# Three of the eight weight sums of a product by thirds move from VectorE to GpSimd

## The chip, the core and the metric

The kernel runs on one core of a Trainium2 chip. Its engines are TensorE (PE in the profile; PEld are its weight loads), VectorE (DVE), ScalarE (ACT), GpSimd (POOL) and SyncE (SP), each with a queue of its own that it works through in order, and 16 DMA engines that all queues share. [...] The metric is the device time of one execution in microseconds (us), the median of several runs.

## What is computed

A graph network of two attention layers over 512 nodes with 768 features and 16,896 edges (8,192 drawn edges, the same turned round, and 512 loops), then a residual and a normalisation:

```python
def gat_layer(x, W, a_s, a_d, b, edge_index, concat):
    n = x.shape[0]
    H, C = a_s.shape
    h = (x @ W).reshape(n, H, C)
    src, dst = (edge_index[0], edge_index[1])
    alpha_s = jnp.einsum('nhc,hc->nh', h, a_s)
    alpha_d = jnp.einsum('nhc,hc->nh', h, a_d)
    e = jax.nn.leaky_relu(alpha_s[src] + alpha_d[dst], NEG_SLOPE)
    m = jax.ops.segment_max(e, dst, num_segments=n)
    e = jnp.exp(e - m[dst])
    denom = jax.ops.segment_sum(e, dst, num_segments=n)
    alpha = e / (denom[dst] + EPS)
    msg = h[src] * alpha[:, :, None]
    out = jax.ops.segment_sum(msg, dst, num_segments=n)
    out = out.reshape(n, H * C) if concat else out.mean(axis=1)
    return out + b
...
h = gat_layer(x, W1, a_src1, a_dst1, b1, edge_list, concat=True)   # 8 heads of 768
h = jax.nn.elu(h)
out = gat_layer(h, W2, a_src2, a_dst2, b2, edge_list, concat=True) # 1 head
...
x = _layernorm(x + out, axis=-1)
```

All data is float32.

## The kernel before

The edges become a dense 512 x 512 matrix of counts, so that attention is a masked softmax over a full matrix and the sum over edges a matrix product. Heads of layer 1 are numbered 0 to 7. For each head the kernel multiplies x by that head's 768 columns of W1 (tiles `hs`), forms the attention matrix (tiles `q`, then `PT`), multiplies it with `hs` (the aggregation), applies ELU (tile `gT`) and multiplies the result by that head's 768 rows of W2, which adds into `h2`. The heads overlap: while head h is aggregated and multiplied by its part of W2, head h+2 is multiplied by its part of W1.

Three schemes with fewer multiplications are used. The aggregation of heads 1 to 5 splits each float32 number into a high and a low part: ScalarE makes the high part (`aH`, L996), VectorE the low part (`aL`, L1000) and their difference (`aD`, L1004), all in tiles named `room`, and TensorE multiplies them (L1044, L1052). Other products are done by quarters. The products with W1 for heads 2 to 7 and with W2 for heads 1 to 7 are done *by thirds*: the 768 x 768 weight is cut in nine blocks of 256 x 256, and fifteen sums and differences of blocks, named P0 to P14, are each multiplied once (W1 products: operations `M.P0` to `M.P14`, L473, emptied into `hs` at L481; W2 products: `m.P0` to `m.P14`, L553, emptied into `h2` at L561).

Of the fifteen weight operands some are raw blocks, some are made by a load on SyncE's queue (L190 for rows, L184 for a block) and an adding DMA on GpSimd's queue (L187: `P1`, `P14`, `P13`, `P12`, `P11`), and eight are made by arithmetic, at L200 in the function `load_thirds`. W1 uses the tiles `w2r` and `w2t`, W2 the tiles `w1r` and `w1t` (swapped for the last head). Each of the eight works on two blocks of 128 x 512 numbers, float32, in SBUF:

- P6 = P14 - P4, then P4 = P13 + P4, P2 = P12 - P13, P10 = P5 + P1, P0 = P12 + P0,
- P1 = P6 + P1, P3 = P10 - P3 and P7 = P6 + P7. P1 overwrites an operand of P10, so it also comes after P10.

There are twelve full sets of eight (six for W1, in the scripts `T.P6` and so on, and six for W2, `w.P6` and so on), and four more in the last head, where the other four sums are made by adding DMAs from SBUF to SBUF (L203).

The order of everything is written by hand. `HEAD`, `REST` and `END` are strings of names, one string for each head, and `run` calls the functions of that name one after the other; each engine's queue then holds its share in that order. Nothing is reordered afterwards. `SPLIT_HEAD` serves heads 1 to 4. Where it makes the sums for W2, it reads:

```python
        dst0 w.P10 A4 D1 aD4 k4 G0 aH2 D4 aH5 w.P6 aL2 aD2 w.P0 d.p12 A2 aL5 v3 v1 G3 aD5 w.P4 k2 v4 w.P1 A5 rooms
        w.P3 G1 G4 m.P2 w.P7 g.P12 k5 D2 D5 v2 dst1 v5 g.P9 swap e.P2 buffers g.P7 d.r3 d.P12 lift2 lift0 next lift1
```

Here `A2` and `A5` are matmuls (L1044) that read what `aH` and `aL` of the same number made, `D` the matmuls (L1052) that read `aD`, `G` writes `gT` (L1061), and `d.P12` is an adding DMA of GpSimd.

Of the kernel before, what the change touches and what calls it, by code (L numbers as in the profile page):

```python
# [37 lines left out]
def gat_pass(  # L38
# [16 lines left out]
    nc = tc.nc  # L55
# [74 lines left out]
    def weight_tile(name, shape):  # L130
        if name not in kept_tiles:
            kept_tiles[name] = wpool.tile([P, *shape], F32, name=name)
        return kept_tiles[name]
# [21 lines left out]
    def square(t_, j):  # L155
        return t_[:, j * 2 * TH:(j + 1) * 2 * TH].rearrange("p (k n) -> p k n", k=2)

    def load_thirds(slot, m, apart):

        def of(rows, k):  # L160
            return rows[k:k + HK + 1:HK] if apart else rows[2 * k:2 * k + 2]

        chunks = list(range(DC))

        def third(k, n):
            ks = of(chunks, k)
            return rows_[:, ks[0]:ks[1] + 1:ks[1] - ks[0], n * TH:(n + 1) * TH]

        def part(k, n):
            cols = slice(n * TH, (n + 1) * TH)  # L170
            if apart:
                return m[:, cols].rearrange("(j k p) d -> k p j d", j=2, p=P)[k]
            return m[k * TH:(k + 1) * TH, cols].rearrange("(k p) d -> p k d", p=P)

        def flat(j):
            return weight_tile(shape=(HK, HALF), name=f"{slot}t{j}").rearrange("p k n -> p (k n)")

        rows_, pair_ = weight_tile(shape=(DC, D), name=f"{slot}r"), flat(1)
        two, four = flat(2), flat(4)
        P13, P12, P11 = square(pair_, 0), square(pair_, 1), square(four, 0)  # L180
        add = ALU.add

        def load(o, k, n):
            return lambda: nc.sync.dma_start(o, part(k, n))  # L184

        def join(o, k, n):
            return lambda: nc.gpsimd.dma_start(o, part(k, n), accum_op=add)  # L187

        def row(k):
            return lambda: nc.sync.dma_start(rows_[:, k, :], m[k * P:(k + 1) * P, :])  # L190

        loads = {f"r{k}": row(k) for k in range(DC)}
        loads.update(P1=join(third(1, 1), 1, 2), P14=join(third(2, 1), 0, 1), p13=load(P13, 0, 2), P13=join(P13, 2, 2),
                     p12=load(P12, 0, 0), P12=join(P12, 1, 0), p11=load(P11, 0, 1), P11=join(P11, 1, 1))
        raw = {(k, n): third(k, n) for k in range(3) for n in range(3)}
        B_ = dict(P8=raw[0, 2], P9=raw[0, 0], P5=raw[0, 1], P13=P13, P12=P12, P14=raw[2, 1], P4=raw[2, 0], P0=raw[1, 2],
                  P3=raw[2, 2], P7=raw[1, 0], P1=raw[1, 1], P6=square(two, 0), P2=square(two, 1), P11=P11, P10=square(four, 1))

        def op(o, a, b, how):
            return lambda: nc.vector.tensor_tensor(B_[o], B_[a], B_[b], op=how)  # L200

        def onto(o, a):
            return lambda: nc.gpsimd.dma_start(B_[o], B_[a], accum_op=add)  # L203
        return B_, loads, dict(
            P6=op("P6", "P14", "P4", ALU.subtract), P4=op("P4", "P13", "P4", add), P2=op("P2", "P12", "P13", ALU.subtract),
            P10=op("P10", "P5", "P1", add), P0=op("P0", "P12", "P0", add), P1=op("P1", "P6", "P1", add),
            P3=op("P3", "P10", "P3", ALU.subtract), P7=op("P7", "P6", "P7", add),
            **{f"q{o}": onto(o, a) for o, a in (("P0", "P12"), ("P4", "P13"), ("P1", "P6"), ("P7", "P6"))})

# [73 lines left out]
    for j in range(2):  # L283
        nc.vector.tensor_reduce(picks[:, j:j + 1], ident.rearrange("p (j k) -> p k j", k=32)[:, j, :], axis=AX.X,
                                op=ALU.add)
# [30 lines left out]
    else:  # L316
# [5 lines left out]
        for c in range(EC):  # L322
            m = (c + 0.5) * P * N / E
            b = int(m // B)
# [1335 lines left out]
```

## Time and profile before

| | before |
|---|---|
| median of 3 runs | 603.82 us (602.72 to 603.88) |
| profiled execution | 604.01 us, span 602.2 us |
| granted TensorE clock, mean | 0.996 |
| TensorE busy | 594.0 us |
| VectorE busy | 534.3 us |
| ScalarE busy | 323.6 us |
| GpSimd busy | 99.0 us, 139 instructions |

The span runs from the first instruction of the program to the last; the time of the execution holds 1.8 us more. "Busy" is the time in which an engine had an instruction; in a row of the timeline stand the start in us from the span's start, the duration, the engine, the line of the kernel, the operation, the tiles written and read, and how many are merged in that row; brackets name the idle time in front of it and what ended it. In rows of groups stand the busy time, the mean of one and the idle time in front.

### The profile page before, as it was taken

To read this page: it belongs to the slowest core of one execution; us is meant where nothing else is said; L and a number is where in the kernel's file an instruction comes from. 1 tells how busy PE (TensorE), PEld (TensorE's weight loads), DVE (VectorE), ACT (ScalarE), POOL (GpSimd) and SP (SyncE) were. 2 spreads that over 40 slices of the span, in tenths; PEclk is the share of its full clock that TensorE was granted. 3 is DMA by queue.
4 is the path that set the end of the run, shared out by engine and by line. 5 is a ranking of instruction groups with operands and counts; after the bars stand their busy time and mean duration, and the time that the engine had idled before them with its cause. 6 is when DMAs were issued, how large, how long until landed. Compare 5 with 4: busy or idle time off the path is not lost.

```text
span 602.2 us, 8248 instructions
## 1 busy us (share of the span) xinstructions
PE 594.0 (99%) x2752; PEld 480.5 (80%) x2752; DVE 534.3 (89%) x1043; ACT 323.6 (54%) x555; POOL 99.0 (16%) x139
## 2 busy tenths in 40 slices
PE   9999999999999999999999999999999999999995
PEld 5666685688888878888888878888888888887863
DVE  7979979768999899988999899989998899899985
ACT  3118774743748164842748255752826347744743
POOL 2210103022012210123011220122021204022000
PEclk9999999999999999999999999999999999999998
DMA  8982899699478977699569987599576959495202
GB/s 296 319 182 71 236 224 278 170 324 223 110 178 191 266 183 208 109 289 213 143 172 179 290 179 214 98 279 233 184 192 166 249 99 257 71 235 98 52 19 107
DMA packets 97341, 114.21 MB, mean 190 GB/s; under 512 B 42966, under 2 KB 78222, under 8 KB 96398
## 3 DMA queue, kind: packets, MB, share of 16 engines
q1 hardware_dynamic: 75230, 89.26, 48.3%
q0 software_dynamic: 21632, 23.79, 25.4%
q10 hardware_dynamic: 432, 0.59, 0.3%
q8 instruction: 23, 0.38, 0.2%
q14 instruction: 24, 0.20, 0.1%
HBM read 99.05 MB, written 2.90 MB: 169 GB/s over the span
## 4 chain that ended last, share of the span: by engine, by line
PE 99%; DVE 0%; ACT 0%; issue 0%; DVEq 0%; ACTq 0%
PE mm L553 23%; PE mm L473 18%; PE mm L414 11%; PE mm L1044 7%; PE mm L1080 5%; PE tr L473 5%; PE bc L553 5%; PE mm L1052 4%; PE tr L553 3%; PE bc L473 3%; PE mm L1475 2%; PE bc L1080 2%; PE tr L1080 2%; PE mm L663 1%; PE bc L1044 1%; PE tr L1044 1%
## 5 line engine op out<-in xcount | busy, mean ns | idle before, releaser
L187 POOL DMA_DIRECT2D w2t<-in_L_gnn_W_dram x21 | 28.4, 1451 | 170.6 <-DMA w2t<-in_L_gnn_W_dram 82.1
L561 DVE TENSOR_TENSOR h<-h,mm 128x512 f32<-128x512 f32 x72 | 49.0, 681 | 8.1 <-PE mm L553 8.0
L703 ACT ACTIVATE q<-q,nmax 128x512 f32<-128x512 f32 x36 | 25.9, 721 | 52.0 <-DVE nmax L700 52.0
L479 ACT ACTIVATE hs<-mm 128x512 f32<-128x512 f32 x23 | 13.6, 593 | 58.5 <-PE mm L473 58.3
L553 PE MATMUL mm<-w1r,gT 128*128 128x256 f32 x176 | 40.4, 379 | 0.0
L928 ACT COPY pS<-q 128x1024 uint16<-128x1024 uint16 x36 | 37.5, 1045 | 0.9
L481 DVE TENSOR_TENSOR hs<-hs,mm 128x512 f32<-128x512 f32 x39 | 26.5, 684 | 12.3 <-PE mm L473 12.1
L553 PE MATMUL mm<-w1r,room 128*128 128x256 f32 x160 | 37.5, 379 | 0.0
L553 PEld LDWEIGHTS mm<-w1r,gT 128*128 128x128 f32 x176 | 33.4, 190 | 4.6
L553 PEld LDWEIGHTS mm<-w1r,room 128*128 128x128 f32 x160 | 30.4, 190 | 4.1
L187 POOL DMA_DIRECT2D w2r<-in_L_gnn_W_dram x14 | 18.6, 1532 | 85.4 <-DVE rden L910 44.0
L187 POOL DMA_DIRECT2D w1t<-in_L_gnn_W_dram x18 | 23.9, 1479 | 45.9 <-DMA w1t<-in_L_gnn_W_dram 39.4
L473 PE MATMUL mm<-w2r,gT 128*128 128x256 f32 x136 | 31.3, 379 | 0.0
L423 DVE SCALAR_TENSOR_TENSOR scr<-hs,a_s 128x768 bf16<-128x768 f32 x32 | 30.5, 953 | 0.4
L423 DVE SCALAR_TENSOR_TENSOR scr<-hs,a_d 128x768 bf16<-128x768 f32 x32 | 30.4, 951 | 0.3
L473 PE MATMUL mm<-w2r,xT 128*128 128x256 f32 x128 | 30.2, 379 | 0.0
L473 PEld LDWEIGHTS mm<-w2r,gT 128*128 128x128 f32 x136 | 25.8, 190 | 3.5
L934 ACT COPY uw<-zr 128x1024 uint16<-128x1024 uint16 x20 | 22.5, 1156 | 9.8 <-DMA zr<-pS 9.8
L473 PEld LDWEIGHTS mm<-w2r,xT 128*128 128x128 f32 x128 | 24.3, 190 | 4.0
L1000 DVE SCALAR_TENSOR_TENSOR room<-room,hs 128x512 fp32r<-128x512 f32 x30 | 20.7, 691 | 7.0 <-ACT room L996 6.8
L695 DVE SCALAR_TENSOR_TENSOR q<-q 128x512 f32<-128x512 f32 x36 | 24.2, 685 | 0.9 <-ACT q L691 0.8
L700 DVE CUSTOM_DVE_ANT_0 q<-q,cnt 128x512 f32<-128x512 f32 x36 | 24.7, 685 | 0.3
(415 smaller groups left out, 1554.7 us busy)
## 6 DMA issues: line engine op xcount, KB each, us to landing
w2r<-in_L_gnn_W_dram SPq DMA_DIRECT2D x48, 384.0 KB
w1r<-in_L_gnn_W_dram SPq DMA_DIRECT2D x43, 384.0 KB
gT<-xd SPq DMA_DIRECT2D x6, 1280.0 KB
w2t<-in_L_gnn_W_dram SPq DMA_DIRECT2D x21, 256.0 KB
w2t<-in_L_gnn_W_dram POOLq DMA_DIRECT2D x21, 256.0 KB, 5.5
w1t<-in_L_gnn_W_dram SPq DMA_DIRECT2D x18, 256.0 KB
w1t<-in_L_gnn_W_dram POOLq DMA_DIRECT2D x18, 256.0 KB, 8.5
w2r<-in_L_gnn_W_dram POOLq DMA_DIRECT2D x14, 256.0 KB, 5.8
```

Of the source, the lines that this page charges most:

```text
L187: return lambda: nc.gpsimd.dma_start(o, part(k, n), accum_op=add)
L414: nc.tensor.matmul(ps[:, :HALF], A_[p][:, k, i * P:(i + 1) * P], B_[p][:, k, :], start=start and k == 0, stop=k == HK - 1, skip_group_chec ...
L423: return [lambda al=al, a=a, sign=sign: nc.vector.scalar_tensor_tensor(scr, HS[h][:, t, :], sign, a, op0=ALU.mult, op1=ALU.mult, accum_out ...
L473: nc.tensor.matmul(bank[chain][:, i * TH:(i + 1) * TH], A_[p][:, k, i * P:(i + 1) * P], B_[p][:, k, :], start=first and i == k == 0, stop= ...
L481: nc.vector.tensor_tensor(out(o), out(o), ps, op=how)
L553: nc.tensor.matmul(bank[chain][:, i * TH:(i + 1) * TH], A_[p][:, k, i * P:(i + 1) * P], B_[p][:, k, :], start=first and i == k == 0, stop= ...
L561: nc.vector.tensor_tensor(out(o), out(o), ps, op=how)
L700: nc.vector.tensor_tensor_reduce(out=q, in0=q, in1=cnt[:, t, :], scale=1.0, scalar=-NO_EDGE / 2, op0=ALU.add, op1=ALU.min, accum_out=nmax)
L703: nc.scalar.activation(q, q, AF.Exp, bias=nmax, scale=-1.0, accum_out=dens[t])
L928: nc.scalar.copy(apart.rearrange("p (h n) -> p h n", h=2), q.bitcast(U16).rearrange("p (n h) -> p h n", h=2))
L1044: nc.tensor.matmul(st["z"][:, :N], A_[c][:, a, s], B_[b][:, s], start=n == s == 0, stop=n == 1 and s == NT - 1, skip_group_check=True)
L1080: nc.tensor.matmul(st[bank][:, :HN], A_[p][:, k, c * P:(c + 1) * P], B_[p][:, k, :], start=start and k == 0, stop=k == 1, skip_group_check ...
```

## The change

Within `load_thirds`, the sums for P1, P3 and P7 are given to GpSimd's queue, at the same places of the hand-written order. The other five stay with VectorE.

```diff
         def op(o, a, b, how):
-            return lambda: nc.vector.tensor_tensor(B_[o], B_[a], B_[b], op=how)
+            engine = nc.gpsimd if o in by_gpsimd else nc.vector
+            return lambda: engine.tensor_tensor(B_[o], B_[a], B_[b], op=how)
+
+        by_gpsimd = ("P1", "P3", "P7")
```

The change adds three lines, so what was L200 is L201, L1000 is L1003, and so on. Two places show what it does to the queues. First GpSimd's queue around the sums for W2 and for W1 of head 1. The tiles `w1t_248` and `w2t_317` hold P6 and P2, `w1t_249` and `w2t_318` hold P11 and P10. Before:

```order
L187 DMA w1r<-in_L_gnn_W_dram 128x2x256 x2
L187 DMA w2t_306<-in_L_gnn_W_dram 128x2x256 x2
L187 DMA w2r<-in_L_gnn_W_dram 128x2x256 x2
L187 DMA w2t_318<-in_L_gnn_W_dram 128x2x256
L187 DMA w1t_118<-in_L_gnn_W_dram 128x2x256 x2
```

and now:

```order
L187 DMA w1r<-in_L_gnn_W_dram 128x2x256 x2
L187 DMA w2t_306<-in_L_gnn_W_dram 128x2x256
L201 TENSOR_TENSOR w1r<-w1t_248,w1r 128x2x256
L201 TENSOR_TENSOR w1r<-w1t_249,w1r 128x2x256
L201 TENSOR_TENSOR w1r<-w1t_248,w1r 128x2x256
L187 DMA w2t_306<-in_L_gnn_W_dram 128x2x256
L187 DMA w2r<-in_L_gnn_W_dram 128x2x256 x2
L201 TENSOR_TENSOR w2r<-w2t_317,w2r 128x2x256
L201 TENSOR_TENSOR w2r<-w2t_318,w2r 128x2x256
L201 TENSOR_TENSOR w2r<-w2t_317,w2r 128x2x256
L187 DMA w2t_318<-in_L_gnn_W_dram 128x2x256
L187 DMA w1t_118<-in_L_gnn_W_dram 128x2x256 x2
```

P1, P3 and P7 of W2 stand between the two adding DMAs into `w2t_306` (P13 and P12 of W1), and P7, P3 and P1 of W1 in front of the adding DMA into `w2t_318` (P11 of W1). Second, VectorE's queue at the first of these places, from P6 on. Before:

```order
L200 TENSOR_TENSOR w1t_248<-w1r 128x512
L1000 SCALAR_TENSOR_TENSOR room<-room,hs 128x512
L1004 TENSOR_TENSOR room<-room 128x512
L200 TENSOR_TENSOR w1r<-w1t_118,w1r 128x2x256
L1000 SCALAR_TENSOR_TENSOR room<-room,hs 128x512
L1061 SCALAR_TENSOR_TENSOR gT<-nr,bc 128x512
L1004 TENSOR_TENSOR room<-room 128x512
L200 TENSOR_TENSOR w1r<-w1t_118,w1r 128x2x256
L200 TENSOR_TENSOR w1r<-w1t_248,w1r 128x2x256
L200 TENSOR_TENSOR w1r<-w1t_249,w1r 128x2x256
L1061 SCALAR_TENSOR_TENSOR gT<-nr,mm_96 128x512
```

and now:

```order
L201 TENSOR_TENSOR w1t_248<-w1r 128x512
L1003 SCALAR_TENSOR_TENSOR room<-room,hs 128x512
L1007 TENSOR_TENSOR room<-room 128x512
L201 TENSOR_TENSOR w1r<-w1t_118,w1r 128x2x256
L1003 SCALAR_TENSOR_TENSOR room<-room,hs 128x512
L1064 SCALAR_TENSOR_TENSOR gT<-nr,bc 128x512
L1007 TENSOR_TENSOR room<-room 128x512
L201 TENSOR_TENSOR w1r<-w1t_118,w1r 128x2x256
L1064 SCALAR_TENSOR_TENSOR gT<-nr,mm_96 128x512
```

From P6 to P4 VectorE's queue is the same; P1 and P3 behind P4 are gone, and P7 a little later.

## The prediction

> **What bounds the kernel now.** I read the page's busy shares first, then the chain that ended last, then busy time by stretches of the span. Two lines of the page:
>
> ```profile
> PE 594.0 (99%) x2752; PEld 480.5 (80%) x2752; DVE 534.3 (89%) x1043; ACT 323.6 (54%) x555; POOL 99.0 (16%) x139
> PE 99%; DVE 0%; ACT 0%; issue 0%; DVEq 0%; ACTq 0%
> ```
>
> The chain is TensorE (PE) from end to end. The stretches say where the missing per cent lies (columns: width, then busy time and count of PE, PEld, DVE, ACT, POOL, granted clock, DMA share, GB/s):
>
> ```profile
> 0.00:10.00 10.00, 8.72 (x32) 5.38 (x33) 7.17 (x17) 2.46 (x4) 3.02 (x57) 1.00 0.79 264
> 140.00:208.00 68.00, 68.00 (x311) 58.38 (x310) 62.72 (x122) 37.54 (x60) 9.38 (x8) 1.00 0.76 196
> 414.00:484.00 70.00, 70.00 (x320) 59.98 (x320) 63.35 (x121) 34.69 (x55) 13.61 (x12) 1.00 0.78 198
> 577.00:602.00 25.00, 18.30 (x60) 10.76 (x59) 18.04 (x43) 9.03 (x20) 0.00 (x0) 0.92 0.17 65
> ```
>
> In the body TensorE is busy all the time at the full clock; its idle time is 1.3 us at the start and 6.7 us in the last 25 us, where no weight sum stands. So nothing taken from VectorE (DVE) can shorten the run by more than crumbs. What can lengthen it is a VectorE result that comes late, and VectorE is 92% busy there (62.72 of 68).
>
> **What the change moves, and its price.** The weight sums as grouped by operation (nanoseconds: minimum, median, maximum):
>
> ```profile
> L200 DVE TENSOR_TENSOR w2r<-w2t,w2r x31: 681/684/693, 115.4 to 554.3; 128x512 f32<-128x512 f32 x31
> L200 DVE TENSOR_TENSOR w1r<-w1t,w1r x30: 650/683/691, 155.0 to 524.9; 128x512 f32<-128x512 f32 x30
> ```
>
> These 61 write into the loaded rows: five sums (P0, P1, P3, P4, P7) in each of twelve sets, and one P3 in the last set. P1, P3 and P7 move: 3 x 12 + 1 = 37. VectorE issues such sums 0.60 us apart (below), so it is relieved of 37 x 0.60 = 22 us; on the path that is worth nothing, since TensorE is what covers it. No DMA is added or removed. The next loads of the rows now also wait for GpSimd's sums, but already waited for the matmuls that read those sums later: nothing.
>
> **GpSimd's price for one sum** is not in the trace: it does no such arithmetic. Nearest rows (GpSimd, by shape; busy us, mean ns, idle before):
>
> ```profile
> L275 POOL IOTA nodes<- 128x512 f16 x1 | 0.6, 553 | 0.4 <-POOLq L1646 0.4
> masks.py:199 POOL TENSOR_SCALAR_AFFINE_SELECT ident<-ident 128x128 f32<-128x128 f32 x1 | 0.3, 294 | 0.1
> L1646 POOL MEMSET const-float32-1.0<- 128x1 f32 x1 | 0.1, 93 | 0.0
> ```
>
> Lower end: VectorE's own 0.68 us. Upper end: the select reads one input, (294 - 93) / 128 = 1.57 ns an element; if each of two inputs cost that, 512 elements take 0.09 + 2 x 0.80 = 1.70 us. I take the middle, 1.2 us. [...]
>
> **Interference between the two engines** is the second unknown, since in the trace GpSimd only fills, generates and issues while VectorE adds. Lower end: VectorE notices nothing. Upper end: a VectorE instruction that comes while a GpSimd sum runs waits for its end. Which one holds decides the sign, because of these rows (VectorE in order of time in head 1, first half; then TensorE):
>
> ```profile
> 153.03 0.68 DVE L200 TENSOR_TENSOR w1t<-w1r 128x512 f32<-128x512 f32 x1
> 153.63 0.69 DVE L1000 SCALAR_TENSOR_TENSOR room<-room,hs 128x512 fp32r<-128x512 f32 x1
> 154.36 0.69 DVE L1004 TENSOR_TENSOR room<-room 128x512 fp32r<-128x512 f32 x1
> 154.97 0.68 DVE L200 TENSOR_TENSOR w1r<-w1t,w1r 128x512 f32<-128x512 f32 x1
> 155.57 0.69 DVE L1000 SCALAR_TENSOR_TENSOR room<-room,hs 128x512 fp32r<-128x512 f32 x1
> 156.17 0.68 DVE L1061 SCALAR_TENSOR_TENSOR gT<-nr,bc 128x512 f32<-128x512 f32 x1
> 156.77 0.69 DVE L1004 TENSOR_TENSOR room<-room 128x512 fp32r<-128x512 f32 x1
> 157.37 1.89 DVE L200 TENSOR_TENSOR w1r<-w1t,w1r 128x512 f32<-128x512 f32 x3
> 160.37 0.68 DVE L200 TENSOR_TENSOR w1r<-w1t,w1r 128x512 f32<-128x512 f32 x1
> ...
> 155.66 1.07 PE L1044 MATMUL tr<-PT,room 128*128 128x512 f32 x4
> 156.57 1.07 PE L1044 MATMUL tr<-pS,room 128*128 128x512 f32 x4
> ```
>
> The first row is P6, the three in one row are P4, P1, P3, the last is P7. P1 and P7 need P6, P3 needs P10, made earlier. VectorE gets to P1, P3 and P7 only at 158 to 161, but GpSimd has nothing else to do and starts P1 as soon as P6 is there, at about 153.7, with P3 and P7 behind it. That is in the middle of the low parts and differences (L1000, L1004), and the L1000 that ends at 155.57 + 0.69 = 156.26 is awaited by the matmul at 156.57: a margin of 0.31 us. With the upper end, P1 starts when the L1000 of 153.63 ends (154.32), ends at 155.52, and the L1004 of 154.36 starts 1.16 us late; nothing has yet been taken from VectorE in front of it. TensorE then stalls 1.16 - 0.31 = 0.85 us, say 0.9. Heads 2 to 4 run the same order; head 4:
>
> ```profile
> 361.13 0.68 DVE L1000 SCALAR_TENSOR_TENSOR room<-room,hs 128x512 fp32r<-128x512 f32 x1
> ...
> 362.10 1.07 PE L1044 MATMUL mm<-pS,room 128*128 128x512 f32 x4
> ```
>
> The margin is again 0.29 us. **Four stalls: 3.6 us.** P3 and P7 collide later, but by then VectorE skips P1, P3, P7 (1.8 us) and catches up.
>
> [...]
>
> Second halves of heads 1 to 4 (the W1 sums): P6 starts at 185.56, and VectorE later idles for TensorE:
>
> ```profile
> 185.56 0.69 DVE L200 TENSOR_TENSOR w2t<-w2r 128x512 f32<-128x512 f32 x1
> 188.70 0.68 DVE L200 TENSOR_TENSOR w2t<-w2r 128x512 f32<-128x512 f32 x1
> 192.32 0.69 DVE L481 TENSOR_TENSOR hs<-hs,mm 128x512 f32<-128x512 f32 x1 [1.04 <-PE mm L473]
> ```
>
> Two collisions cost at most 2.4 us; P7 and P3 leave VectorE (1.2 us) and 1.04 us of idle time follow. **Nothing**, and if that cover were gone, about 0.9 us a head. Head 5, second half:
>
> ```profile
> 465.83 0.94 DVE L967 TENSOR_TENSOR room<-hs 128x768 f32<-128x768 f32 x1
> 468.18 0.69 DVE L481 TENSOR_TENSOR hs<-hs,mm 128x512 f32<-128x512 f32 x1 [0.80 <-PE mm L473]
> 468.78 0.95 DVE L969 TENSOR_TENSOR hs<-hs 128x768 f32<-128x768 f32 x1
> 470.52 0.68 DVE L481 TENSOR_TENSOR hs<-hs,mm 128x512 f32<-128x512 f32 x1
> ...
> 471.43 1.89 PE L473 MATMUL mm<-w2r,xT 128*128 128x256 f32 x8
> ```
>
> A delay at 465.83 is lost again in the 0.80 us of idle time; one at 468.78, when GpSimd is at P7 and P1, is not: 1.1 us less the margin of 471.43 - 471.20 = 0.23: **0.9 us**. Head 6 has P7 and P3 behind GpSimd's copy at 511.39:
>
> ```profile
> 511.39 1.21 POOL L203 DMA_DIRECT2D w2r<-w2t  x1 [3.58 <-DVE gT L586]
> 512.21 0.69 DVE L586 TENSOR_TENSOR gT<-room,gT 128x512 f32<-128x512 f32 x1 [0.17 <-PE mm L553]
> 512.82 0.68 DVE L561 TENSOR_TENSOR h<-h,mm 128x512 f32<-128x512 f32 x1
> ...
> 513.73 1.46 PE L553 MATMUL mm<-w1t,gT 128*128 128x256 f32 x6
> ```
>
> Margin 0.23 us, so **0.9 us** once more. Head 0, head 5's first half and the end I put together at 0.3 us. Sum: 3.6 + 0.9 + 0.9 + 0.3 = 5.7 us at the upper end of interference. The profiled execution took 604.01 us (span 602.2 and 1.8 around it), 0.2 above the median of 603.82: 604.0 + 5.7 - 0.2 = **609.5 us**. With a sum at 0.68 us the stalls shrink by 0.5 each, to about 2.7 us in all (606.5); at 1.70 us they grow by 0.5, to about 9 us (613). I choose the upper end of interference because the two engines read the same tiles at the same instants, and because one side of the unknown is nearly closed: TensorE has no idle time to win.
>
> **Rivals.** (1) *No interference, or VectorE always goes first.* Then the sums only come at other times. Their matmuls stand 5 to 33 us behind in nearly all places, GpSimd reaches them earlier than VectorE did, and the time stays at 603.8, perhaps half a us less. For it speaks that VectorE's sums vary only from 650 to 693 ns although GpSimd issues 80 DMAs meanwhile; against it, that these read no tile. It decides as soon as a delay of VectorE stays under 0.3 us.
>
> (2) *GpSimd's queue.* Its DMAs with addition now stand behind sums that wait for P6 and P10. The tightest (head 1, GpSimd's row, its time to landing, and the matmul that reads it):
>
> ```profile
> 189.31 1.20 POOL L187 DMA_DIRECT2D w2t<-in_L_gnn_W_dram  x1 [12.96 <-DVE hs L481]
> DMA to landing us min/median/max: 10.8/11.1/11.3
> 205.94 1.89 PE L473 MATMUL bc<-w2t,gT 128*128 128x256 f32 x8
> ```
>
> P10 ends at 189.38, then P3 and P1: the issue moves to 189.4 + 2 x 1.2 = 191.8, the landing to 203. The margin is 5.5 us and 2.5 are used, so it decides only when a sum takes over 2.7 us. At 3.5 us it would cost 1.5 us in each of five heads, 7.5 in all: 611.
>
> (3) *Faster.* The relief of 22 us would have to meet waits of TensorE on VectorE. The body has none that the stretches show; half a us at most, plus luck: 602.4.
>
> **Chances.** Interference 0.60, none 0.28, the queue 0.06, faster 0.06. A change within 0.2% (1.2 us) is about what cannot be told from none: faster 0.06, same 0.28, slower 0.66. The range runs from 603.2, which takes in most of the case of no interference, to 614.0, past the upper price; the likeliest case alone has 606.5 to 613.
>
> **What would show it.** In the changed profile: sums on GpSimd of 1.0 to 1.7 us, P1 starting right behind P6; in heads 1 to 4 the L1003 and L1007 rows (the old L1000 and L1004) around P1 stretched or with a gap of about 1.2 us; TensorE's busy rows there with gaps of 0.9 us before the matmul on room; the accumulated load still landed ahead of its matmul. I am wrong if VectorE's rows keep their 0.60 us spacing beside GpSimd's sums, or if the sums on GpSimd are long because they do the waiting.

## The result, and the profile after

The changed kernel takes 628.46 us (median of 4 runs, 625.4 to 630.8), the kernel before 603.34 us beside it (4 runs, 602.72 to 603.88). The ratio is 1.041, with a 95% interval of 1.036 to 1.047: 25 us slower. The prediction said slower, by 6 us, and with a range that ended at 614.0 us. The profiled execution took 630.8 us, its span 629.0 us, 26.8 us more than before.

From the page of the changed kernel, busy time and the shares of the chain that ended last:

```profile
PE 601.8 (96%) x2752; PEld 483.1 (77%) x2752; DVE 546.4 (87%) x1006; ACT 324.2 (52%) x555; POOL 155.5 (25%) x176
PE 82%; DVE 10%; DMA 4%; issue 2%; SPq 1%; ACT 1%; DVEq 0%; ACTq 0%
```

The chain was TensorE alone; now VectorE has a tenth of it. VectorE lost 37 instructions, which were worth 22 us of its queue (37 starts, 0.60 us apart), and is busy 12 us longer. The sums themselves, grouped by operation (nanoseconds: minimum, median, maximum):

```profile
L201 POOL TENSOR_TENSOR w2r<-w2t,w2r x19: 1259/1712/2922, 114.8 to 568.5; 128x512 f32<-128x512 f32 x19
L201 POOL TENSOR_TENSOR w1r<-w1t,w1r x18: 1662/1719/1763, 153.1 to 533.4; 128x512 f32<-128x512 f32 x18
L201 DVE TENSOR_TENSOR w1r<-w1t,w1r x12: 651/683/1769, 155.3 to 510.8; 128x512 f32<-128x512 f32 x12
```

A GpSimd sum takes 1.26 us where nothing is in its way and about 1.72 us mostly; VectorE's own sum takes 0.68 us, and up to 1.77 us. Now the place of which the prediction spoke, head 1, first half: VectorE, then GpSimd, then TensorE.

```profile
152.34 0.69 DVE L201 TENSOR_TENSOR w1t<-w1r 128x512 f32<-128x512 f32 x1
152.94 0.69 DVE L1003 SCALAR_TENSOR_TENSOR room<-room,hs 128x512 fp32r<-128x512 f32 x1
153.67 1.67 DVE L1007 TENSOR_TENSOR room<-room 128x512 fp32r<-128x512 f32 x1
155.26 1.77 DVE L201 TENSOR_TENSOR w1r<-w1t,w1r 128x512 f32<-128x512 f32 x1
156.95 1.75 DVE L1003 SCALAR_TENSOR_TENSOR room<-room,hs 128x512 fp32r<-128x512 f32 x1
158.62 0.68 DVE L1064 SCALAR_TENSOR_TENSOR gT<-nr,bc 128x512 f32<-128x512 f32 x1
...
153.12 5.03 POOL L201 TENSOR_TENSOR w1r<-w1t,w1r 128x512 f32<-128x512 f32 x3 [14.17 <-DVE w1t L201]
...
154.94 1.07 PE L1047 MATMUL tr<-PT,room 128*128 128x512 f32 x4
158.75 2.08 PE L1047 MATMUL tr<-pS,room 128*128 128x512 f32 x4 [2.75 <-DVE room L1003]
```

GpSimd does its three sums back to back (one row of 5.03 us), and each of them holds one of the three next VectorE rows: 1.67, 1.77 and 1.75 where 0.69, 0.68 and 0.69 stood before. Together they are 3.1 us longer than before. Less the margin of 0.31 us, that is about the 2.75 us for which TensorE's matmul on `room` waits. Its four matmuls then take 2.08 us where they took 1.07: the granted clock has fallen to half. The stretch behind it, those of the same matmul in heads 2 and 3, and one in head 6 (width, PE, PEld, DVE, ACT, POOL busy, clock, DMA share, GB/s):

```profile
158.00:165.00 7.00, 6.25 (x15) 4.96 (x16) 3.69 (x6) 1.90 (x3) 1.29 (x2) 0.51 0.25 37
233.00:237.00 4.00, 3.76 (x10) 3.05 (x11) 3.18 (x6) 1.89 (x3) 1.20 (x1) 0.57 0.44 67
306.00:310.00 4.00, 3.63 (x16) 3.10 (x17) 3.31 (x6) 1.78 (x3) 1.20 (x1) 1.00 0.44 68
536.00:541.00 5.00, 4.64 (x14) 3.79 (x15) 4.83 (x11) 2.36 (x3) 0.00 (x0) 0.66 0.00 0
```

In heads 1, 2 and 6 the clock is down (0.51, 0.57, 0.66 over these stretches), in head 3 it is not. Head 6 has the longest hold. VectorE, GpSimd and TensorE there:

```profile
531.58 4.13 DVE L589 TENSOR_TENSOR gT<-room,gT 128x512 f32<-128x512 f32 x1 [0.17 <-PE mm L556]
...
531.44 1.21 POOL L206 DMA_DIRECT2D w2r<-w2t  x1 [3.00 <-DMA w2t<-in_L_gnn_W_dram]
532.19 2.96 POOL L201 TENSOR_TENSOR w1r<-w1t,w1r 128x512 f32<-128x512 f32 x2
...
536.36 3.24 PE L556 MATMUL mm<-w1t,gT 128*128 128x256 f32 x8 [3.10 <-DVE h L564]
```

Here one VectorE row of 4.13 us (0.69 before) outlasts both sums, which follow directly on a GpSimd DMA. Head 5's first half has the same, behind the DMA at 453.41:

```profile
453.94 3.75 DVE L592 SCALAR_TENSOR_TENSOR room<-gT 128x512 f32<-128x512 f32 x1
...
453.41 1.20 POOL L187 DMA_DIRECT2D w2t<-in_L_gnn_W_dram  x1 [6.76 <-DMA w2t<-in_L_gnn_W_dram]
454.18 2.95 POOL L201 TENSOR_TENSOR w1r<-w1t,w1r 128x512 f32<-128x512 f32 x2
```

To split the loss, I paired TensorE's 2,752 matmuls of both traces one to one and subtracted their starts. A stall costs its idle time and 0.2 to 0.3 us more. The last matmul comes 27.3 us later; the span is 26.8 us longer, so 0.5 us of that is made up behind it:

| place | predicted | idle of TensorE | later by |
|---|---|---|---|
| heads 1 to 4, matmul on `room` | 4 x 0.9 | 2.75, 2.75, 2.74, 2.74 | 12.1 |
| heads 1 to 4, second halves | 0 | none | 0 |
| head 5, first half | within 0.3 | 1.86 | 2.2 |
| head 5, second half | 0.9 | 0.84 | 1.1 |
| head 6 | 0.9 | 3.10 | 3.3 |
| the end | within 0.3 | 2.14 and 0.32 | 2.9 |
| half clock behind three of the stalls | none | - | 6.2 |
| the start, and drift | - | - | -0.5 |
| sum | 5.7 | | 27.3 |

### The profile page after: what moved, and what is told of

It is laid out like the page before. It is cut to its first block, busy times and chain, and to the rows that moved or that the text cites. A ratio compares the mean times of both kernels' runs of the same rounds, so it can differ in the third digit from the quotient of the medians.

```text
span 629.0 us, 8307 instructions
## 1 busy us (share of the span) xinstructions
PE 601.8 (96%) x2752; PEld 483.1 (77%) x2752; DVE 546.4 (87%) x1006; ACT 324.2 (52%) x555; POOL 155.5 (25%) x176
## 4 chain that ended last, share of the span: by engine, by line
PE 82%; DVE 10%; DMA 4%; issue 2%; SPq 1%; ACT 1%; DVEq 0%; ACTq 0%
PE mm L556 21%; PE mm L476 17%; PE mm L417 10%; PE tr L476 5%; PE bc L556 5%; PE mm L1083 4%; PE tr L556 3%; PE bc L476 3%; PE mm L1047 2%; PE mm L1478 2%; DMA w2r<-in_L_gnn_W_dram 2%; DVE room L1003 2%; PE mm L1055 2%; PE bc L1083 2%; DVE room L1007 2%
## 5 line engine op out<-in xcount | busy, mean ns | idle before, releaser
L201 POOL TENSOR_TENSOR w2r<-w2t,w2r 128x512 f32<-128x512 f32 x19 | 30.4, 1636 | 76.6 <-issue 42.7
L201 POOL TENSOR_TENSOR w1r<-w1t,w1r 128x512 f32<-128x512 f32 x18 | 29.6, 1717 | 59.2 <-DVE w1t L201 59.2
L1047 PE MATMUL mm<-pS,room 128*128 128x512 f32 x88 | 24.9, 406 | 8.2 <-DVE room L1003 8.2
L187 POOL DMA_DIRECT2D w1t<-in_L_gnn_W_dram x18 | 25.6, 1669 | 24.4 <-PE mm L556 13.4
L1003 DVE SCALAR_TENSOR_TENSOR room<-room,hs 128x512 fp32r<-128x512 f32 x30 | 25.2, 838 | 6.9 <-ACT room L999 6.8
L187 POOL DMA_DIRECT2D w1r<-in_L_gnn_W_dram x12 | 15.0, 1330 | 55.6 <-DMA w1r<-in_L_gnn_W_dram 43.4
L556 PE MATMUL mm<-w1t,gT 128*128 128x256 f32 x96 | 25.7, 416 | 3.1 <-DVE h L564 3.1
```

The source lines that it names most:

```text
L201: return lambda: engine.tensor_tensor(B_[o], B_[a], B_[b], op=how)
L556: nc.tensor.matmul(bank[chain][:, i * TH:(i + 1) * TH], A_[p][:, k, i * P:(i + 1) * P], B_[p][:, k, :], start=first and i == k == 0, stop= ...
L1003: return lambda: nc.vector.scalar_tensor_tensor(parts[c][:, 1], parts[c][:, 0].bitcast(F32), SPLIT, HS[h][:, :, c * P:(c + 1) * P], op0=AL ...
L1047: nc.tensor.matmul(st["z"][:, :N], A_[c][:, a, s], B_[b][:, s], start=n == s == 0, stop=n == 1 and s == NT - 1, skip_group_check=True)
```

## Experiments

The theory that these rows suggest, called *turns*: a VectorE instruction with two inputs in SBUF waits for the end of a GpSimd sum that runs, and the engines then alternate, so that n sums in a row delay n VectorE instructions. The rivals: GpSimd's queue (its adding DMAs come late, or someone waits for its results); a fixed price wherever the sums stand; a shared limit of SBUF; and the clock as a cause of its own.

**1 and 2: one kind of set alone.** The W1 sets, then the W2 sets on GpSimd (`apart` is true for W2).

```diff
-        by_gpsimd = ("P1", "P3", "P7")
+        by_gpsimd = () if apart else ("P1", "P3", "P7")      # W1 sets
+        by_gpsimd = ("P1", "P3", "P7") if apart else ()      # W2 sets
```

> GpSimd forms P1, P3 and P7 in the six sets for W1 alone; VectorE keeps all eight sums of the sets for W2. Theory of turns (a VectorE instruction with two inputs in SBUF waits for the end of a GpSimd sum that is running, and the two engines then alternate): second halves of heads 1 to 4 lie under waits of TensorE's making and cost nothing, head 5's second half costs the 0.84 us seen there in the changed kernel, the low clock does not come; 604 to 605 us, within 0.3% of before. Queue theory (GpSimd's adding DMAs come late behind sums that wait): half of the sums and half of the delay, so about half of the 25 us, 614 us.

> GpSimd forms P1, P3 and P7 in the sets for W2 alone (and in the last head's); VectorE keeps all eight of the sets for W1. Theory of turns: the stalls of 2.75 us in each of heads 1 to 4 stay (11 us), those of head 5's first half (1.9), head 6 (3.1) and the end (2.5) too as far as these are sums for W2, with the phases of low clock: 622 to 628 us. Queue theory: about 614 us.

W1 sets: 604.81 us against 603.71 (ratio 1.0021, 1.0011 to 1.0031), 1.1 us, as expected. The only wait of TensorE on VectorE in the body is head 5's, in the row of waits (total, times, longest):

```profile
PE mm L476 <- DVE hs L484: 0.8, 1, 0.8
```

W2 sets: 627.74 us (1.0397, 1.0350 to 1.0443), 24.0 us, as expected. The two add up to the whole change's 25.1 us, though each has nearly half of the sums: 18 cost 1 us, 19 cost 24. What counts is where a sum stands. This is against a price for each sum and against the queue theory, which had 614 us for both.

**3: P1 alone on GpSimd.**

```diff
+        by_gpsimd = ("P1",)
```

> GpSimd forms P1 alone, in all sets; P3 and P7 are VectorE's again. Theory of turns with three sums in a row: one GpSimd sum holds one VectorE instruction, so the stall of heads 1 to 4 shrinks from 2.75 us to about 1.1 - 0.3 = 0.8 us each, 3.2 us in all, head 6 and the end 0 to 2 us, and no stall is long enough to lower the clock: 606 to 609 us. Rival, one long hold whatever the number of sums (a fixed price for GpSimd's first sum): the stalls of heads 1 to 4 stay near 2.7 us, 620 us or more. If collisions were only counted and their place did not matter: a third of 25 us, 612 us.

607.55 us (1.0066, 1.0049 to 1.0083), as expected. Head 1 again, VectorE, GpSimd, TensorE:

```profile
153.68 1.67 DVE L1007 TENSOR_TENSOR room<-room 128x512 fp32r<-128x512 f32 x1
155.27 0.68 DVE L201 TENSOR_TENSOR w1r<-w1t,w1r 128x512 f32<-128x512 f32 x1
155.88 0.68 DVE L1003 SCALAR_TENSOR_TENSOR room<-room,hs 128x512 fp32r<-128x512 f32 x1
...
153.13 1.67 POOL L201 TENSOR_TENSOR w1r<-w1t,w1r 128x512 f32<-128x512 f32 x1 [13.94 <-DVE w1t L201]
...
156.61 1.21 PE L1047 MATMUL tr<-pS,room 128*128 128x512 f32 x4 [0.59 <-DVE room L1003]
```

One sum, one stretched row, and a stall of 0.59 us in each of the four heads, which makes TensorE 0.9 us later there. The prediction had a stall of 0.9 us here, for three sums.

**4: the same sums later.** In heads 1 to 4 P6, for which all three W2 sums wait directly or through the queue, moves behind the last low part.

```diff
-... aH2 D4 aH5 w.P6 aL2 aD2 w.P0 ... G3 aD5 w.P4 ...
+... aH2 D4 aH5 aL2 aD2 w.P0 ... G3 aD5 w.P6 w.P4 ...
```

> The changed kernel, with P6 of the sets for W2 moved in the order of heads 1 to 4 from ahead of the low part aL2 to behind the difference aD5, so that GpSimd's three sums start behind the low parts that TensorE waits for; the number of sums is the same. Theory of turns at that place: the four stalls of 2.75 us in heads 1 to 4 go (11 us) with the phases of low clock there (5 us), while head 5, head 6 and the end keep theirs (8 us and 1.7 us of clock): 612 to 616 us. Queue theory, or a price of the sums themselves wherever they stand: 626 to 630 us, like the changed kernel.

610.92 us (1.0117, 1.0100 to 1.0134): 17.5 us less than the changed kernel with the same 37 sums. The four stalls are gone: the matmul on `room` follows its neighbour at 155.91 us in head 1, and the sums first meet `gT` rows that read PSUM.

```profile
155.91 1.07 PE L1047 MATMUL tr<-pS,room 128*128 128x512 f32 x4
...
157.48 4.73 POOL L201 TENSOR_TENSOR w1r<-w1t,w1r 128x512 f32<-128x512 f32 x3 [18.14 <-DVE w1t L201]
...
158.03 1.28 DVE L1064 SCALAR_TENSOR_TENSOR gT<-nr,mm 128x512 f32<-128x512 f32 x2
```

It came out 1 us under the expected range because head 6's stall of 3.10 us, where nothing was edited, is gone too: GpSimd's two sums there now held another VectorE row (L698, 2.36 us), behind which TensorE does not stall. The stalls of head 5 (1.62 and 0.85 us) and of the end (2.14 us) stay.

**5: extra sums that nobody reads.** VectorE keeps all its sums.

```diff
+                if o in ("P1", "P3", "P7"):
+                    nc.gpsimd.tensor_tensor(spare.rearrange("p (k n) -> p k n", k=2), B_["P6"], B_["P6"], op=add)
+                nc.vector.tensor_tensor(B_[o], B_[a], B_[b], op=how)
```

> The kernel before, with VectorE still forming all eight sums; added are 37 sums on GpSimd (P6 + P6, at the places of P1, P3 and P7) into a tile that nobody reads. Theory of turns: the stalls come as in the changed kernel although nothing waits for GpSimd's sums, and are somewhat longer since VectorE keeps its 22 us of sums: 625 to 640 us. Rival, late results (TensorE or VectorE waits for what GpSimd made, or for its adding DMAs): nobody waits for the tile, 603.7 to 606 us.

624.07 us (1.0349, 1.0333 to 1.0365) against 603.48. Nobody waits for these sums, and the slowdown is nearly that of the change, so it comes neither from a dependency nor from late results. Head 1, VectorE:

```profile
154.35 1.41 DVE L1010 TENSOR_TENSOR room<-room 128x512 fp32r<-128x512 f32 x1
155.69 1.52 DVE L205 TENSOR_TENSOR w1r<-w1t,w1r 128x512 f32<-128x512 f32 x1
157.13 1.52 DVE L1006 SCALAR_TENSOR_TENSOR room<-room,hs 128x512 fp32r<-128x512 f32 x1
```

The same three rows, each some 0.25 us shorter than in the changed kernel: a sum of a tile with itself takes GpSimd 1.03 us alone (measured in experiment 9), not 1.25. Together they are 2.4 us longer than in the kernel before; less the margin of 0.31 us that makes a stall of 2.1 us by estimate, where the same sum gives 2.8 for the changed kernel (2.75 measured). The mean clock of the profiled run was 0.995 instead of 0.987. Both fit a result 1 us under the range; how much each gave was not measured.

**6: as much work on GpSimd, but hardly any reading.** At the same places one column is copied (which waits for P6) and a tile filled three times.

```diff
+                if o in ("P1", "P3", "P7"):
+                    nc.gpsimd.tensor_copy(dot, B_["P6"][:, 0, :1])
+                    for _ in range(3):
+                        nc.gpsimd.memset(spare, 0.0)
```

> The kernel before, with VectorE still forming all eight sums; at each place of P1, P3 and P7 GpSimd gets a copy of one column that waits for P6, and three fills of a 128x512 tile that nobody reads, so it is occupied as long as by a sum and its queue is delayed as much, but hardly reads SBUF. If reading SBUF on both sides is what collides: 603.7 to 605 us. If GpSimd's queue (late adding DMAs) or any work on GpSimd slows the rest: 615 us or more. If writes of GpSimd collide with VectorE as reads do: 620 us or more.

603.46 us against 603.48 (1.0002, 0.9993 to 1.0012). GpSimd is as occupied (three fills take 1.69 us) and its DMAs stand behind as much, and nothing happens. VectorE's row beside the fills (GpSimd's below) keeps its length:

```profile
153.71 0.69 DVE L1012 TENSOR_TENSOR room<-room 128x512 fp32r<-128x512 f32 x1
...
153.65 1.69 POOL L206 MEMSET spare<- 128x512 f32 x3
```

This closes the prediction's second rival: the adding DMAs have room enough.

**7: the two engines by themselves.** A kernel of its own with chains on 128x512 float32 tiles, of VectorE or ScalarE beside GpSimd (in outline):

```python
sums()                                                 # 4 x gpsimd.tensor_tensor(po, c, d)
for _ in range(12): vector.tensor_tensor(dv, a, b)     # or (dv, a, psum tile), tensor_copy, scalar.activation
```

> A kernel of its own, which computes nothing of the reference: ten stretches, in which VectorE (or ScalarE) runs a chain of 128x512 instructions, alone or beside four GpSimd instructions. Theory of turns: VectorE's addition of two SBUF tiles 0.60 to 0.69 us alone, GpSimd's 1.26 us alone; together VectorE's rows 1.6 to 1.8 us while a sum runs, GpSimd's 1.7; beside sums VectorE's additions with one input in PSUM stay at 0.6 to 0.7 us, and so do ScalarE's copies; beside fills VectorE stays at 0.6 to 0.7; beside GpSimd copies of one input it stretches. Behind a GpSimd DMA with two sums, one VectorE row is held through both, 3 to 4 us. Rival, a shared limit of SBUF: all rows beside a sum get longer by the same few tens of per cent, whatever they read, ScalarE's too.

In order: VectorE's addition alone, GpSimd's alone, the two together, VectorE with one input in PSUM, VectorE's copy from SBUF, ScalarE's copy, VectorE's addition beside GpSimd fills, and beside GpSimd copies:

```profile
L42 DVE TENSOR_TENSOR dv<-a,b x8: 680/692/693, 5.5 to 10.6; 128x512 f32<-128x512 f32 x8
L46 POOL TENSOR_TENSOR po<-c,d x4: 1255/1260/1262, 11.9 to 15.9; 128x512 f32<-128x512 f32 x4
L42 DVE TENSOR_TENSOR dv<-a,b x4: 1632/1634/1658, 17.4 to 22.5; 128x512 f32<-128x512 f32 x4
L58 DVE TENSOR_TENSOR dv<-a,ps x12: 678/687/689, 30.6 to 38.5; 128x512 f32<-128x512 f32 x12
L62 DVE COPY dv<-a x4: 1366/1368/1391, 39.9 to 44.2; 128x512 f32<-128x512 f32 x4
L74 ACT ACTIVATE ac<-a x12: 613/629/630, 69.9 to 77.2; 128x512 f32<-128x512 f32 x12
L42 DVE TENSOR_TENSOR dv<-a,b x12: 683/692/693, 49.9 to 57.9; 128x512 f32<-128x512 f32 x12
L42 DVE TENSOR_TENSOR dv<-a,b x4: 980/982/984, 59.3 to 62.4; 128x512 f32<-128x512 f32 x4
```

Four sums stretch exactly four VectorE additions, by 0.94 us each, although the two engines read different tiles (`a` and `b`, `c` and `d`); the additions with a PSUM input (0.678 to 0.689 us) and ScalarE's copies (0.613 to 0.630 us) keep their length beside them. A shared limit of SBUF would have touched them too: that rival falls. A copy of VectorE, which reads one SBUF tile, is held as well (1.37 us; the last copies of that chain, without a sum beside them, took 0.43). One part of the expectation was missed: behind a DMA the longest row was 2.16 us, not 3 to 4. There both sums write one tile; experiment 9 gives each its own.

**8: the stalls filled.** The changed kernel; TensorE multiplies zeros into the same accumulator while it would wait in heads 1 to 4.

```diff
+                    if n == 1 and c == 5 and h < 5:
+                        for _ in range(12):
+                            nc.tensor.matmul(st["z"][:, :N], nought[:, :P], nought, start=False, stop=False, ...)
```

> The changed kernel; in heads 1 to 4 TensorE gets twelve multiplications of zeros (128x512, about 0.2 us each) ahead of the matmul that waits 2.75 us for the low part, so that it is not idle there. The stalls stay in time, the multiplications lie in them. If the low clock follows from TensorE's idle time: no half clock at the first two of these places, 5 us less than the changed kernel's profiled run, and runs closer together, 623 to 626 us. If the low clock has another cause: 628 us, with the same spread of 625 to 631.

624.08 us (5 runs, 623.96 to 625.18; ratio 1.0346, 1.0332 to 1.0360), 4.4 us less than the changed kernel and with a spread of 1.2 us instead of 5.4. Head 1, TensorE (eleven of the twelve have a record), and the clock of the same stretch:

```profile
156.27 2.54 PE L1050 MATMUL tr<-nought 128*128 128x512 bf16 x11
158.96 1.19 PE L1052 MATMUL tr<-pS,room 128*128 128x512 f32 x4 [0.16 <-DVE room L1005]
...
158.00:165.00 7.00, 6.84 (x31) 5.35 (x30) 6.07 (x11) 3.88 (x7) 1.51 (x2) 1.00 0.27 37
```

The matmul on `room` still starts at 159 us, but at full clock (1.00 where 0.51 stood). Head 6's stall was not filled, and the clock stayed full there (1.00 from 531 to 536 us). The mean clock was 0.997 in all five runs, and 0.987, 0.995, 0.986 and 0.994 in the four of the changed kernel, the two longest of which are the two with the lowest clock. So the half clock in heads 1 to 4 is a consequence of TensorE's idle time, and the changed kernel's spread goes with it.

**9: behind a DMA.** A second kernel of its own: VectorE's chain beside GpSimd sums that write tiles of their own, with a GpSimd DMA ahead of them or not (in outline).

```python
gpsimd.dma_start(half, source, accum_op=ADD)           # ahead of the sums, behind them, or absent
for j in range(3): gpsimd.tensor_tensor(own[j], c, d)
for _ in range(12): vector.tensor_tensor(dv, a, b)
```

> A kernel of its own, which computes nothing of the reference: VectorE runs chains of twelve additions of two SBUF tiles (128x512) beside two or three GpSimd sums that write tiles of their own, with a GpSimd DMA directly ahead of the sums, behind them, or absent. If GpSimd's issue of a DMA lets parts of it run ahead into the next sums, so that there is no instant between two sums at which VectorE gets in: without a DMA ahead each of three sums stretches one VectorE row to 1.6 to 1.8 us; with a DMA directly ahead one row takes 3 us or more for two sums and 4 us or more for three; a DMA behind the sums does nothing. If the long rows of 3.75 and 4.13 us have another cause (the instruction's kind, the tiles): rows of 1.6 to 2.2 us in all stretches. The sum of a tile with itself: 0.9 to 1.0 us if reading one tile is cheaper, else 1.26 us.

VectorE's rows: three sums without a DMA, three behind an adding DMA, two behind one from SBUF to SBUF, three behind a plain DMA, two behind an adding DMA but with a one-column copy in between that waits for VectorE, and three with the DMA behind them:

```profile
L44 DVE TENSOR_TENSOR dv<-a,b x3: 1632/1633/1662, 7.3 to 10.6; 128x512 f32<-128x512 f32 x3
L44 DVE TENSOR_TENSOR dv<-a,b x12: 691/693/5431, 19.5 to 32.2; 128x512 f32<-128x512 f32 x12
L44 DVE TENSOR_TENSOR dv<-a,b x12: 682/692/3202, 33.6 to 44.1; 128x512 f32<-128x512 f32 x12
L44 DVE TENSOR_TENSOR dv<-a,b x11: 683/692/4384, 57.0 to 68.0; 128x512 f32<-128x512 f32 x11
L44 DVE TENSOR_TENSOR dv<-a,b x3: 692/1634/1777, 48.4 to 51.0; 128x512 f32<-128x512 f32 x3
L44 DVE TENSOR_TENSOR dv<-a,b x3: 1633/1634/1656, 70.1 to 73.4; 128x512 f32<-128x512 f32 x3
```

Without a DMA ahead each of the three sums holds one VectorE row (1.63 to 1.66 us). Directly behind each of the three kinds of DMA, one VectorE row is held through all the sums (5.43, 3.20, 4.38 us) and the others keep their 0.69; with the copy between DMA and sums, which waits 1.9 us for VectorE, the turns are back (rows of 1.63 and 1.78 us; whether by the wait or by the time that passes, this run does not tell). This is head 6's row of 4.13 us, shown apart from the kernel. The sum of a tile with itself took 1.03 us, just over the expected 0.9 to 1.0.

**10: only the harmless places.** The W1 sets that are made in heads 0 to 4 on GpSimd (15 of 37 sums): the places that no stall followed so far.

```diff
+        by_gpsimd = ("P1", "P3", "P7") if hidden else ()
...
+            B3, loads3, T = load_thirds("w2", w1[:, (h + 2) * D:(h + 3) * D], False, h < 5)
```

> GpSimd forms P1, P3 and P7 only in the five sets for W1 of heads 0 to 4, whose collisions fall where VectorE afterwards idles for TensorE (15 sums of 37). Theory of turns: VectorE's rows are stretched there as in the changed kernel, but no stall of TensorE follows: 603 to 604.2 us, not to be told from before. If every collision cost time wherever it stands: 15 of 37 of 25 us, 613 us. If the relief of VectorE by 9 us were worth anything: under 602.5 us.

603.91 us (11 runs) against 603.62; ratio 1.0009, 1.0000 to 1.0018: no difference that can be told with certainty, and no gain. VectorE's rows are stretched as before, and then VectorE waits for TensorE (head 1, second half):

```profile
186.68 1.76 DVE L589 TENSOR_TENSOR room<-gT 128x512 f32<-128x512 f32 x1
...
197.21 0.69 DVE L484 TENSOR_TENSOR hs<-hs,bc 128x512 f32<-128x512 f32 x1 [2.49 <-PE bc L476]
```

VectorE gives up 15 sums, but its busy time is 534.5 us where it was 534.3: the stretched rows take back what the sums had cost. So this run does not show what a relief of VectorE by itself would be worth. No version that I ran beats the kernel before.

## Why the prediction was right in kind and wrong in size

**No gain to be had: right.** TensorE was busy all through the body of the kernel before, and no placement of the sums brought a gain. That the relief alone is worth nothing is inferred from that; experiment 10 does not test it, since VectorE's busy time stayed the same.

**GpSimd's price, 1.2 us: right, in part by luck.** A sum takes 1.26 us by itself; the prediction had taken the middle between two distant rows, 0.68 and 1.70 us. The rows of 1.72 us in the kernel contain the wait for a VectorE instruction: head 1's three take 5.03 us together, where three times 1.26 are 3.8. One of the prediction's signs of being wrong was that GpSimd's sums are long because they do the waiting: they do wait, 0.4 us each by these numbers, but VectorE waits too.

**The upper end of interference: right.** In experiment 7 a VectorE addition of two SBUF tiles that met a GpSimd sum took 1.63 us against 0.69 alone, one beside GpSimd's fills 0.69, and one with an input in PSUM beside sums 0.69. The first rival, no interference, falls. The prediction's reason for this choice was not the right one: it was that the two engines read the same tiles, and in experiment 7 they read different ones and collide all the same.

**The step that failed: "P3 and P7 collide later, but by then VectorE skips P1, P3, P7 (1.8 us) and catches up."** They do not collide later. GpSimd has all three sums ready behind P6, so they come back to back and take turns with VectorE's next three instructions, all of which stand ahead of the matmul on `room`. The term 4 x 0.9 = 3.6 us was one collision of three; it measured 12.1 us. For one collision its size was right by luck: experiment 3 has 0.59 us of idle time where the prediction worked out 0.85, and the 0.3 us that a stall costs beyond its idle time, which the prediction did not have, make it 0.9 again. The relief, on which the step counted, lies behind P4, after the harm: at the time when the low part `aL5` is due, VectorE's queue is the same as before.

**Head 5, first half, head 6 and the end: 1.2 us predicted, 8.4 measured.** For head 6 the prediction had one collision less its margin; the two sums held one row together behind GpSimd's DMA. So did they in head 5's first half (3.75 us). The end was not worked out at all; 0.3 us was put down for it and two other places. There one GpSimd sum of 2.92 us, behind three GpSimd DMAs, held two VectorE rows (2.46 and 2.01 us).

**Head 5, second half: right**, 0.9 predicted, 0.84 us idle. **Second halves of heads 1 to 4: right**, nothing.

**The clock: not thought of**, 6.2 us in the profiled run. It came behind stalls of 2.75, 2.75 and 3.10 us; with 0.9 us each it would probably not have come, since the four runs of experiment 3, with stalls of 0.59 us, have a mean clock of 0.996 to 0.999, like the kernel before.

**The second rival, GpSimd's queue: rightly small**; experiments 5 and 6 exclude it.

## What to carry to other kernels

Before moving work between VectorE and GpSimd, look at what VectorE does *while* GpSimd runs it: here each GpSimd sum of 128x512 held one VectorE instruction with two SBUF inputs (1.63 us instead of 0.69) or one copy from SBUF (1.37 instead of 0.43), three ready sums held three, and directly behind a GpSimd DMA three held one through all of them (5.43 us). Count collisions from the instant at which the whole queue becomes ready, against the margin of the first result that the bounding engine awaits, and count the relief only from where it stands in the queue. Such work belongs beside instructions that read PSUM (in experiment 7 they kept 0.69 us beside the sums), or where VectorE waits anyway, and even there it gained nothing here, with TensorE as the bound (603.91 us against 603.62 in experiment 10).

## What the runs showed of the hardware

- A VectorE copy of a float32 tile in SBUF (0.43 us) is held by a GpSimd sum like an addition of two tiles (1.37 us), and a GpSimd copy holds VectorE too (0.98 instead of 0.69 us).
- Directly behind a GpSimd DMA, GpSimd's sums held one VectorE instruction for up to 5.43 us. That row begins at 19.50 us, before the first sum's own row does, at 20.23:

```profile
19.33 1.32 POOL L58 DMA_DIRECT2D wide<-in_x_dram  x1
20.23 4.14 POOL L50 TENSOR_TENSOR own<-c,d 128x512 f32<-128x512 f32 x3
```

  Behind the plain DMA GpSimd's three sums take 3.71 us together, about their length alone (three times 1.26), so only VectorE waits there, where three sums without a DMA take 4.59 us. Why the row is held through all of them was not shown.
- Idle times of TensorE of 2.75 us halved the clock in heads 1 and 2 of the changed kernel (for 6.8 and 3.4 us) and not, with 2.74 us, in heads 3 and 4. The length alone does not decide: behind 2.14 us of idle time at the end of experiment 4 five matmuls took 2.50 us, where eight of the same size had taken 1.89 us ahead of it, so the clock was about half by estimate, and behind 2.14 us at the end of the changed kernel the clock was full (1.00 from 575 to 580 us). In the trace of the changed kernel the granted clock changes at 158.08, 164.91, 233.18 and 236.59 us and later. The times between its changes are 6.83, 68.27, 3.41, 300.37, 3.41 and 85.33 us, that is 2, 20, 1, 88, 1 and 25 times 3.413 us. So where an idle time lies between two such instants may matter; this was not tested, and what decides stays open.
